# Routing the first 12 token tiles during attention and running four expert slots beside the routing of all tokens

## The chip, the cores and the metric

The kernel runs on one core of one Trainium2 chip. The metric is the device time of one execution in microseconds; the kernel before took 2799.47 us (median of three runs, 2798.77 to 2800.43). The core's engines are TensorE (PE in the profile), VectorE (DVE), ScalarE (ACT), GpSimd (POOL) and SyncE (SP), which here only issues DMAs. Each engine runs its own instructions in order and waits for others by semaphores.

## The reference

One image of 256 channels and 64 x 64 pixels goes through two layers: a windowed linear attention with a residual, and then, on its 4096 pixels as tokens, full attention with 8 heads and a mixture of experts. All is float32. The last part is the one that matters here:

```python
t = t + attn(layernorm(t))                 # 8 heads of 32, 4096 tokens
z = layernorm(layernorm(t))                # outer one is the expert's own, with gain and shift
logits = layernorm(t) @ Wr + br            # 8 experts
p, idx = top_k(softmax(logits), 2); w = p / p.sum()
y[e] = gelu((z * ln_g[e] + ln_b[e]) @ W1[e] + b1[e]) @ W2[e] + b2[e]   # 256 -> 1024 -> 256
out = t + w[0] * y[idx[0]] + w[1] * y[idx[1]]
```

Only the two chosen experts of each token count, so 8192 rows are computed instead of 32768.

## The kernel before

The tokens lie in 32 tiles of 128 (`t`, with eight more columns per token that hold the router's products). After the first layer, the part of the second layer that matters is in three stages.

**Attention.** 16 rounds (8 chunks of 512 queries, two groups of four heads), of 32 steps, one per tile of keys. In a step PE makes the scores of four heads (L1144) into one bank (`ps_one`) and a set of three banks (`three_banks`, two sets), ACT takes their exponentials (L1153, L1156) into one of eight weight buffers, and PE, two steps later, multiplies them with the values (L1103). DVE adds most weight buffers up for the denominators (`add`, L1175); every fourth step from 5 on a DMA from POOL's queue adds one instead (L1164). At given steps of a round other work is put in: `gather` at 5, `pack` at 9 (the last round's denominators, L1205, then DMAs on SP's queue), `turn` at 17, `spread` at 29, and in odd rounds from the third on two groups of output projections at 13 and 25 (`some_projections`, L1081), which also take a set of three banks, add to `t` (L1085) and make the statistics of the second norm (L151, L152). The whole stands in the true branch of a condition on the size of the scores; the false branch is a slower form of attention that these inputs do not take.

**Routing.** After the branch all 32 tiles are routed at once: two norms (ACT has the square roots), the normalised rows written to DRAM (`zrows`, L1398 on ACT and L1402 on SP), the logits and the two best experts on DVE (L1412 to L1433), counts before each token by two products on PE (L1436, L1438), and from these, on DVE, each token's position in its expert's list. Positions count in units of 128 rows; a slot is two units, 256 rows of one expert. The lists (which token stands at a position) come from an inversion: for each tile a one-hot matrix of positions within a unit (`line`, L1536) is multiplied with one of units (`piece`, L1538 to L1540), 64 products in 8 chunks (L1542). `owners` gives the expert of each slot (`expert_of`), and the last lines the row numbers to gather from (`source`) and to scatter to (`target`).

**Experts.** `run` goes through 32 slots of 256 rows and 4 of 128 (between them). For a slot, SP loads the expert's weights (L1366 to L1369, the expert's number read from `expert_of`), POOL issues gathers of the rows (L1582), PE transposes them (L1597), DVE applies gain and shift (L1601); then eight pairs of products with a Gelu each (L1622, L1625) and sixteen with the second layer's weights (L1631), DVE adds the bias (L1633) and POOL issues the scatters into `yrows` (L1634). The next slot's loads and transposes are issued one slot ahead. A conditional tail (`more_slots`) runs further single slots if the lists need them. A last stage weighs the two rows of each token, adds and transposes.

The order of instructions on each engine is made by a scheduler from the order in the code, dependences and its own estimates; `tc.issue_after(x)` holds an instruction behind another. Tiles of a later pool lie on memory of closed pools, and their first use waits for the last uses there.

Of the kernel before, what the change touches and what calls it, by code (L numbers as in the profile page):

```python
# [30 lines left out]
P = 128  # L31
# [18 lines left out]
NS = 2 * N // SLOT  # L50
NU = 2 * NS + NE
USUAL = 2 * NS + NE // 2
TAME = 60.0
# [9 lines left out]
    "m": {"rank": NE, "iota": P, "before": P, "ones": P, "number": 1, "high": 2 * NT, "spare": NU, "unit": NS + NE, "least": 2 * NE},  # L63
# [8 lines left out]
def constants():  # L72
# [32 lines left out]
    out[:, _AT["spare"]] = 1 + 2 * N + p[:, None] + P * np.arange(NU)[None, :]  # L105
    out[:, _AT["unit"]] = np.concatenate([2 * np.arange(NS), 2 * NS + np.arange(NE)])
# [5 lines left out]
def tile_conv_attn_hybrid(ctx: ExitStack, tc: tile.TileContext, a: dict, out: bass.AP):  # L112
# [771 lines left out]
    crows = e_dram.tile([NE, P, NH + 2 * KC], F32, name="crows")  # L884

# [13 lines left out]
    with ExitStack() as phase:  # L899
# [189 lines left out]
        with tc.If(tame > 0) as branch:  # L1089
            with (  # L1090
# [138 lines left out]

                def some_projections(n):  # L1230
                    tiles = list(range(len(done), len(done) + n))
                    done.extend(tiles)
                    pr = three_banks()
                    project([pr[:, j] for j in range(n)], tiles, lambda k, i: result(k, i // NB)[:, tok(i % NB)])

                for s, (r, i) in enumerate(places):
# [16 lines left out]
                    if s < len(places) - 2:  # L1253
                        add(r, i)

# [13 lines left out]
        with branch.Else():  # L1269


            with (
# [45 lines left out]
                for i in range(NT):  # L1318
                    project([ps.tile([P, CH], F32, tag="sc", name="ps_sc")], [i], lambda k, i: attnT[:, k, tok(i)])

# [5 lines left out]
    with ExitStack() as phase:  # L1326
# [7 lines left out]
        root = small.tile([1, 1], F32, name="root")  # L1334
        nc.scalar.sqrt(root, ident[:1, :1])
        cst.update(constants_of("m", wts))
        zrows = dram.tile([N, C], F32, name="zrows")
        yrows = dram.tile([2 * N + NU * P, C], F32, name="yrows")

# [12 lines left out]
        expert_of = small.tile([P, NS + NE], mybir.dt.int32, name="expert_of")  # L1352
# [4 lines left out]
        def weights(work, s):  # L1357

            e = nc.values_load(
                expert_of[:1, s : s + 1], engines=(mybir.EngineType.SP,), min_val=0, max_val=NE - 1  # L1360
            )
# [4 lines left out]
            nc.sync.dma_start(cols, crows[bass.ds(e, 1)].rearrange("o p n -> p (o n)"))  # L1366
            nc.sync.dma_start(w1, a["L1_ffn_W1"][bass.ds(e, 1)].rearrange("o (k p) h -> p (o k) h", p=P))
            nc.sync.dma_start(w2, a["L1_ffn_W2"][bass.ds(e, 1)].rearrange("o (k p) d -> p (o k) d", p=P))
            nc.sync.dma_start(b2, a["L1_ffn_b2"][bass.ds(e, 1)].rearrange("o d -> (o d)").partition_broadcast(P))  # L1369
# [5 lines left out]
        slot_work = experts.enter_context(tc.tile_pool(name="m_work", bufs=2))  # L1375

        with ExitStack() as routing:
            pool = lambda name, bufs: routing.enter_context(tc.tile_pool(name=name, bufs=bufs))
            r_ps = routing.enter_context(psum("r_ps", 2))
# [3 lines left out]


            norm = norm2
            norm.begin(0, NT)
            norm.end(0, NT)
            again = one("again")
            nc.vector.tensor_mul(again, norm.var, norm.rstd)
            nc.vector.tensor_mul(again, again, norm.rstd)  # L1390
            again = rstd_of(small, again, NT, 1e-5)
            nc.vector.tensor_mul(again, again, norm.rstd)
            less = one("less")
            nc.vector.scalar_tensor_tensor(less, norm.mean, -1.0, again, op0=ALU.mult, op1=ALU.mult)

            z = act.rearrange("p k n -> p (k n)").rearrange("p (i c) -> p i c", c=C)
            for i in range(NT):
                nc.scalar.activation(  # L1398
                    z[:, i, :], t[:, i, :C], AF.Identity, scale=again[:, i : i + 1], bias=less[:, i : i + 1]
                )  # L1400
                if i % 8 == 7:
                    nc.sync.dma_start(  # L1402
                        zrows[P * (i - 7) : P * (i + 1), :].rearrange("(i p) c -> p i c", p=P),
                        z[:, i - 7 : i + 1, :],
                    )

            on_experts = lambda v: v.unsqueeze(2).to_broadcast([P, NT, NE])
            on_tiles = lambda v: v.unsqueeze(1).to_broadcast([P, NT, NE])  # L1410
            logit = each("logit")
            nc.vector.tensor_mul(logit, on_experts(norm.mean), on_tiles(wr_sum))  # L1412
            nc.vector.tensor_sub(logit, t[:, :, C:], logit)
            nc.vector.tensor_mul(logit, logit, on_experts(norm.rstd))
            nc.vector.tensor_add(logit, logit, on_tiles(br))

            rank = on_tiles(cst["rank"])
            hots, most = [], [one(f"most{n}") for n in range(2)]
            for n in range(2):
                first, hot, place = each(f"first{n}"), each(f"hot{n}"), one(f"place{n}")  # L1420
                hots.append(hot)
                nc.vector.tensor_reduce(most[n], logit, AX.X, ALU.max)
                nc.vector.tensor_tensor(first, logit, on_experts(most[n]), ALU.is_equal)
                nc.vector.tensor_mul(first, first, rank)
                nc.vector.tensor_reduce(place, first, AX.X, ALU.max)
                nc.vector.tensor_tensor(hot, first, on_experts(place), ALU.is_equal)
                if n == 0:

                    nc.vector.scalar_tensor_tensor(logit, hot, -1e30, logit, op0=ALU.mult, op1=ALU.add)


            chosen = small.tile([P, NE, NT], F32, name="chosen")
            nc.vector.tensor_add(chosen.rearrange("p e i -> p i e"), hots[0], hots[1])  # L1433
            flat = lambda v: v.rearrange("p e i -> p (e i)")
            counts = bank()
            nc.tensor.matmul(counts[:, : NE * NT], cst["before"], flat(chosen), start=True, stop=True)  # L1436
            sums = bank()
            nc.tensor.matmul(sums[:, : NE * NT], cst["ones"], flat(chosen), start=True, stop=True)  # L1438
# [4 lines left out]
            nc.vector.tensor_copy(flat(per_tile), sums[:, : NE * NT])  # L1443
# [3 lines left out]


            iota = cst["iota"]
            total = upto[:, :, NT - 1]  # L1450
# [27 lines left out]

# [3 lines left out]
            nc.vector.tensor_scalar_mul(begins, begins, float(P))  # L1482

            def owners():


                past = small.tile([P, NS + NE, 2 * NE], F32, name="past")
                nc.vector.tensor_tensor(
                    past,
                    cst["unit"].unsqueeze(2).to_broadcast([P, NS + NE, 2 * NE]),  # L1490
                    ends.rearrange("p n e -> p (n e)").unsqueeze(1).to_broadcast([P, NS + NE, 2 * NE]),
                    ALU.is_ge,
                )
                owner = small.tile([P, NS + NE], F32, name="owner")
# [8 lines left out]
            by_tile = lambda v: v.unsqueeze(2).to_broadcast([P, NE, NT])  # L1503
            rest = small.tile([P, NE, NT], F32, name="rest")
# [3 lines left out]
            nc.vector.tensor_add(row, row, rest)  # L1508

# [5 lines left out]
            back = bank("acc")  # L1518
            for n in range(2):
                at = each(f"at{n}")  # L1520
                nc.vector.tensor_mul(at, hots[n], row.rearrange("p e i -> p i e"))
                pos = one(f"pos{n}")
                nc.vector.tensor_reduce(pos, at, AX.X, ALU.add)
                whole, part = (small.tile([P, NT], I32, name=f"{x}{n}") for x in ("whole", "part"))
                which, within = (small.tile([P, NT], BF16, name=f"{x}{n}") for x in ("which", "within"))
                nc.vector.tensor_copy(whole, pos)
                nc.vector.tensor_single_scalar(part, whole, P - 1, op=ALU.bitwise_and)
# [188 lines left out]
```

## Time and profile before

| | |
|---|---|
| median of three runs | 2799.47 us |
| the profiled execution, its own time | 2798.76 us |
| its span | 2797.0 us |
| PE busy | 2658.0 us (95%) |
| DVE busy | 1855.3 us (66%) |
| ACT busy | 1516.9 us (54%) |
| POOL busy | 812.0 us (29%) |
| last attention instruction on DVE ends | 2212.3 us |
| first product of an expert slot | 2262.6 us |

A busy share is of the whole span. A timeline line has start, length, engine, line of the code, operation, tiles (out<-in), shapes and how many instructions were merged; in brackets the idle time of the engine before it and what ended it. "issue" is idle time for which the profile shows no cause. A window line gives the busy time of each engine in a stretch, the clock that TensorE was granted (1.00 is full), the busy share of the DMA engines and the bytes moved.

### The profile page before, as it was taken

The numbers are of one execution on the slowest core, as the hardware profiler recorded it, in microseconds if no ns is written. First come the engines' busy times: TensorE is split into PE (matmuls) and PEld (weight loads), VectorE is DVE, ScalarE is ACT, GpSimd is POOL, SyncE is SP. The second block draws the span as 40 slices with busy tenths as digits, with TensorE's granted clock in tenths as the row PEclk, the third lists the DMA queues.
The fourth block names the chain that finished last, engine by engine and source line by source line (L and its number), as shares of the span: only waits on it lengthen the run. The fifth ranks groups of instructions, "written<-read, shape, count | busy, mean of one in ns | idle before, by whom it ended". The sixth has DMA issues, their size and how long they took to land.

```text
span 2797.0 us, 72047 instructions
## 1 busy us (share of the span) xinstructions
PE 2658.0 (95%) x31078; PEld 1216.5 (43%) x31078; DVE 1855.3 (66%) x2434; ACT 1516.9 (54%) x2117; POOL 812.0 (29%) x914
## 2 busy tenths in 40 slices
PE   6889999998999999999999999999999689999996
PEld 5454336645433655111212122222222168888884
DVE  6758788575878876888888888888888721111114
ACT  3222323222332334999898989999999622222222
POOL 2057777305777741100000000000000022222220
PEclk9999999999999999999999999999999889999997
DMA  5000000000000000555555555555555356656665
GB/s 143 6 23 25 11 28 21 8 12 23 25 11 28 21 21 2 112 120 113 109 120 109 118 111 111 111 118 109 120 109 113 94 185 208 198 197 199 208 214 191
DMA packets 120587, 265.77 MB, mean 95 GB/s; under 512 B 20386, under 2 KB 81416, under 8 KB 106180
## 3 DMA queue, kind: packets, MB, share of 16 engines
q0 software_dynamic: 22368, 133.18, 22.4%
q1 hardware_dynamic: 90724, 118.95, 13.1%
q10 hardware_dynamic: 7168, 8.92, 0.9%
q8 instruction: 248, 4.06, 0.6%
q14 instruction: 79, 0.65, 0.1%
HBM read 127.56 MB, written 18.12 MB: 52 GB/s over the span
## 4 chain that ended last, share of the span: by engine, by line
PE 92%; DVE 3%; issue 2%; DMA 2%; ACT 0%; POOL 0%; SPq 0%; ACTq 0%; DVEq 0%; POOLq 0%
PE ps_three L1144 18%; PE ps_acc L1103 18%; PE ps_hp L1622 8%; PE ps_yp L1631 8%; PE ps_sc L817 8%; PE ps_acc L833 7%; PE ps_sc L717 3%; PE ps_sc L744 3%; PE ps_acc L775 3%; PE ps_two L402 2%; PE ps_two L435 2%; PE ps_mm L988 2%; PE ps_two L516 1%; PE ps_acc L763 1%; PE ps_three L1081 1%
## 5 line engine op out<-in xcount | busy, mean ns | idle before, releaser
L1144 PE MATMUL ps_three<-qk 32*64 32x512 f32 x6144 | 563.3, 612 | 2.2 <-DVE t L1085 1.2
L1144 PE MATMUL ps_one<-qk 32*64 32x512 f32 x2048 | 556.7, 613 | 0.2 <-ACT pe L1153 0.2
L1175 DVE TENSOR_TENSOR act<-act,pe 128x2048 f32<-128x2048 f32 x195 | 446.8, 2291 | 97.2 <-ACT pe L1156 62.5
L637 ACT COPY sm<-ps_sc 128x384 f32<-128x384 f32 (+3 forms) x454 | 218.4, 510 | 527.2 <-PE ps_sc L817 338.8
L1156 ACT ACTIVATE pe<-ps_three 128x1536 f32<-128x1536 f32 x330 | 477.4, 1447 | 0.0
L644 DVE TENSOR_TENSOR sm<-ps_sc,mask 128x512 f32<-128x512 f32 (+3 forms) x740 | 340.1, 519 | 68.9 <-PE ps_sc L817 65.7
L644 POOL TENSOR_TENSOR sm<-sm,mask 128x192 f32<-128x192 f32 (+3 forms) x428 | 349.7, 846 | 113.9 <-ACT sm L637 113.6
L1175 DVE TENSOR_TENSOR act<-act 128x2048 f32<-128x2048 f32 x150 | 343.8, 2292 | 56.0 <-ACT act L1156 42.5
L1164 POOL DMA_DIRECT2D pe<-pe x108 | 92.9, 860 | 954.0 <-ACT pe L1156 666.7
L1103 PE MATMUL ps_acc<-pe,v 128*32 128x512 f32 x2640 | 351.6, 605 | 0.0
L1625 ACT ACTIVATE hid<-ps_hp,cols 128x256 f32<-128x256 f32 (+1 forms) x288 | 133.0, 462 | 360.4 <-PE ps_hp L1622 359.3
L1144 PEld LDWEIGHTS ps_three<-qk 32*64 32x64 f32 x6144 | 112.6, 129 | 414.9 <-ACT pe L1153 244.0
L1156 ACT ACTIVATE act<-ps_three 128x1536 f32<-128x1536 f32 x182 | 263.1, 1446 | 0.0
L1622 PE MATMUL ps_hp<-xe,w 128*128 128x256 f32 (+1 forms) x1152 | 246.1, 370 | 0.0
L1631 PE MATMUL ps_yp<-w,hid 128*128 128x256 f32 x1088 | 240.8, 379 | 0.0
L817 PE MATMUL ps_sc<-qk 32*64 32x384 f32 (+3 forms) x3584 | 234.6, 458 | 0.1
L1153 ACT ACTIVATE pe<-ps_one 128x512 f32<-128x512 f32 x330 | 197.3, 598 | 59.5 <-PE ps_one L1144 35.2
L644 POOL TENSOR_TENSOR sm<-sm,ycut 128x384 f32<-128x384 f32 (+4 forms) x146 | 147.2, 1029 | 256.8 <-ACT sm L637 256.5
L1622 PEld LDWEIGHTS ps_hp<-xe,w 128*128 128x128 f32 x1152 | 200.9, 190 | 39.4 <-ACT hid L1625 5.3
L1631 PEld LDWEIGHTS ps_yp<-w,hid 128*128 128x128 f32 x1088 | 204.2, 190 | 26.4
L833 PE MATMUL ps_acc<-sm,v 128*32 128x256 f32 (+3 forms) x2688 | 213.2, 419 | 0.1
L1601 DVE TENSOR_SCALAR xe<-ps_tp,cols 128x256 f32<-128x256 f32 (+1 forms) x72 | 34.8, 525 | 240.8 <-PE ps_tp L1597 217.1
(270 smaller groups left out, 3008.0 us busy)
## 6 DMA issues: line engine op xcount, KB each, us to landing
pe<-pe POOLq DMA_DIRECT2D x108, 1024.0 KB, 7.4
w<-in_L_ffn_W SPq DMA_DIRECT2D x72, 1024.0 KB
by<-recs SPq DMA_DIRECT2D x48, 256.0 KB
b<-in_L_ffn_b SPq DMA_DIRECT2D x36, 128.0 KB
rows<-in_x SPq DMA_DIRECT2D x16, 256.0 KB
zrows<-act SPq DMA_DIRECT2D x4, 1024.0 KB
y<-yrows ACTq DMA_DIRECT2D x8, 512.0 KB
y<-yrows SPq DMA_DIRECT2D x8, 512.0 KB
```

The costliest lines, as they stand in the source:

```text
L637: copied = nc.scalar.copy(sm[:, :used], sc[:, :used])
L644: done = engine.tensor_mul(to, of, mk.unsqueeze(1).to_broadcast(list(to.shape)))
L817: nc.tensor.matmul(scs[h][u : u + rows, at : at + n], kT[hs[h], P * i + u : P * i + u + rows], qT[hs[h], CH * ix + CELL * c0 : CH * ix + C ...
L833: nc.tensor.matmul(acc[hs[h], CELL * c0 : CELL * c1], v[:, i, hs[h]], sms[h][:, at : at + n], start=not begun[0], stop=last and at == plac ...
L1103: nc.tensor.matmul(to[D * hd : D * (hd + 1), :], lhsT(hd), rhs(hd), start=start, stop=stop, skip_group_check=True,)
L1144: nc.tensor.matmul(to[CELL * u : CELL * (u + 1), :], qk[hs, 1, g, P * i + CELL * u : P * i + CELL * (u + 1)], qk[hs, 0, g, chunk(qc)], sta ...
L1153: first = nc.scalar.activation(head(pe, 0), one, AF.Exp, scale=C**-0.5)
L1156: nc.scalar.activation(pe[:, CH:], three.rearrange("p h n -> p (h n)"), AF.Exp, scale=C**-0.5).ins
L1175: latest[:] = [nc.vector.tensor_add(total, total, weights_of[r, i]).ins]
L1622: nc.tensor.matmul(hp[:, :n], w1[:, k, tok(m)], x_now[:, k, :n], start=k == 0, stop=k == KC - 1)
L1625: nc.scalar.activation(hid[:, m, :n], hp[:, :n], AF.Gelu, bias=cols[:, m : m + 1])
L1631: nc.tensor.matmul(yp, hid[:, m, tok(j)], w2[:, m, :], start=m == 0, stop=m == NH - 1)
```

## The change

Three things change together.

A function `early_routing` routes the first 12 tiles and only for experts 0 to 3, in 18 parts that are put at steps of attention's rounds 8 to 14, each behind DVE's latest addition. It works in the memory of queries that those rounds no longer need. It makes `lists`, the rows of the first 256 tokens of each of the four experts, and writes the normalised rows of these tiles to `zrows`. Inverse square roots are made on DVE by an integer guess and three Newton steps (`rsqrts`) in place of ACT's square root, here and in the full routing.

The expert stage then has 4 early slots (experts 0 to 3, number known while the program is written), 28 full and 4 half slots. `run` has become a generator that stops after each pair of first-layer products and each half of second-layer products, and the routing code advances it in between: slot 0 up to the counts, slot 1 up to the inversion, slot 2 through the inversion, a piece after each chunk. The remaining 20 tiles' rows are scaled on ACT after the Gelus of slots 0 to 2 (`beside`). Early slots have gain and shift applied by ACT instead of DVE.

The full routing leaves out the rows that the early slots have taken (`gone`), and the sigmoid of the two weights is taken after the last Gelu.

```diff
+EARLY = 4
+ETILES = 12
-NS = 2 * N // SLOT
+NS = 2 * N // SLOT - EARLY
...
+    def rsqrts(x, y, part):
+        bits = y.bitcast(I32)
+        nc.vector.tensor_single_scalar(bits, x.bitcast(I32), 1, op=ALU.arith_shift_right)
+        nc.vector.tensor_scalar(bits, bits, -1.0, float(0x5F3759DF), op0=ALU.mult, op1=ALU.add)
+        for _ in range(3):
+            nc.vector.scalar_tensor_tensor(part, y, -0.5, y, op0=ALU.mult, op1=ALU.mult)
+            nc.vector.tensor_mul(part, part, x)
+            nc.vector.scalar_tensor_tensor(y, part, 1.5, y, op0=ALU.add, op1=ALU.mult)
...
+    def early_routing(spaces, banks):
...
+        def count():
+            of = banks(2)
+            for z, by in zip(of, ("before", "ones")):
+                nc.tensor.matmul(z[:, : E * M], c[by], flat(chosen), start=True, stop=True)
...
+        def invert():
+            (z,) = banks(1)
+            for n in range(2):
+                for i in range(M):
+                    nc.tensor.matmul(
+                        z[:, : 4 * E].rearrange("p (m n) -> p m n", m=2),
+                        line[n][:, :, i],
+                        piece[n][:, 1:, :, i],
...
+        def scaled(i):
+            to = staged[i // 2 % 2]
+            for j in range(2):
+                at = slice(i + j, i + j + 1)
+                nc.vector.tensor_scalar(
+                    to[:, j], t[:, i + j, :C], y[:, 1, at], less[:, at], op0=ALU.mult, op1=ALU.add
+                )
+            nc.sync.dma_start(zrows[P * i : P * (i + 2), :].rearrange("(i p) c -> p i c", p=P), to)
+
+        parts = [load, norms, top_one, top_two, count, ranks, lambda: place_of(0), lambda: place_of(1)]
+        parts += [lambda: one_hots(0), lambda: one_hots(1), invert, finish]
+        parts += [lambda i=i: scaled(i) for i in range(0, M, 2)]
+        return parts
...
+                spaces = [qk[:, 0, g, : 4 * CH] for g in range(KC)]
+                early = early_routing(spaces, some_banks)
+                when = [(8, 13), (8, 21), (8, 25), (9, 9), (9, 21), (10, 9), (10, 13), (10, 21), (10, 25), (11, 9), (11, 21), (12, 9)]
+                when += [(12, 13), (12, 21), (12, 25), (13, 9), (13, 21), (14, 9)]
...
+                    if (r, i) in early:
+                        with tc.issue_after(latest[0]):
+                            early[r, i]()
...
+                rows, n = (lists[:, 0], P * ETILES) if slot[0] is not None else (source, N)
...
+                    if by_scalar:
+                        nc.scalar.activation(
+                            xe[:, k, :n], tp[:, k, :n], AF.Identity, scale=cols[:, gain], bias=cols[:, shift]
+                        )
...
+                    if beside and (slot[0] or m >= NH // 2):
+                        with tc.issue_after(done["gelu"]):
+                            beside.pop(0)()
+                    yield
...
+        usual = [(e, 2 * e, 2 * e + 1) for e in range(EARLY)]
...
+            two_norms(0, NT, x, y, part, less)
+            rstd, again = y[:, 0], y[:, 1]
+            advance(1)
...
+            beside.extend(lambda i=i: scaled(i) for i in range(ETILES, NT))
...
+            advance(9)
...
+            with tc.issue_after(done["product"]):
+                nc.tensor.matmul(counts[:, : NE * NT], cst["before"], flat(chosen), start=True, stop=True)
+                nc.tensor.matmul(sums[:, : NE * NT], cst["ones"], flat(chosen), start=True, stop=True)
...
+            with tc.issue_after(done["y"]):
+                nc.vector.tensor_copy(flat(per_tile), sums[:, : NE * NT])
...
+            advance(10)
...
                     if n == 0 and i8 == G:
                         with tc.issue_after(made.ins):
                             owners()
-
+                    advance(1)
+
+            advance(2)
...
+        for _ in work_on:
+            pass
         experts.close()
+        with tc.issue_after(done["gelu"]):
+            for n in range(2):
+                nc.scalar.activation(top[n], top[n], AF.Sigmoid)
```

## The prediction, made before the result

> **What bounds the kernel now.** I read the slices first, then windows of 10 us where the slices dip, then the timeline there, and last the timeline of attention. The slices (70 us each; the page's second part) show TensorE at nine tenths nearly everywhere, with a dip in the 32nd, where its clock is also down:
>
> ```profile
> PE   6889999998999999999999999999999689999996
> DVE  6758788575878876888888888888888721111114
> PEclk9999999999999999999999999999999889999997
> ```
>
> The windows over that dip: start and end, length, busy us of PE, weight loads, DVE, ACT, POOL (instructions in brackets), granted clock, DMA share, GB/s.
>
> ```profile
> 2210.00:2220.00 10.00, 0.62 (x3) 0.19 (x1) 6.70 (x28) 1.45 (x4) 0.04 (x1) 0.67 0.01 3
> 2220.00:2230.00 10.00, 2.05 (x4) 1.18 (x4) 7.31 (x25) 10.00 (x22) 0.00 (x0) 0.50 0.52 177
> 2230.00:2240.00 10.00, 3.87 (x15) 2.31 (x16) 9.27 (x29) 8.35 (x16) 0.00 (x0) 0.50 0.72 244
> 2240.00:2250.00 10.00, 10.00 (x39) 5.42 (x38) 7.02 (x14) 3.44 (x5) 0.00 (x0) 0.50 0.77 237
> 2250.00:2260.00 10.00, 4.36 (x17) 2.17 (x15) 1.90 (x10) 2.06 (x2) 3.63 (x4) 0.50 0.69 241
> ```
>
> For about 52 us, from 2210.6 to 2262.6, TensorE does only the routing's own small products, at half clock: a serial stage. The timeline (start, us, engine, line, operation, tiles; idle before and what ended it) gives its links:
>
> ```profile
> 2157.39 2.05 PE L1081 MATMUL ps_three<-wo,act 128*128 128x264 f32 x8
> 2212.01 0.30 DVE L152 BATCH_NORM_AGGREGATE ln_mv<-st 128x2 f32<-128x6 f32 x2
> 2215.23 0.18 DVE L1452 TENSOR_SCALAR steps<-cstm 128x16 f32<-128x16 f32 x1 [2.92 <-issue]
> 2223.28 1.19 PE L1436 MATMUL ps_mm<-chosen,cstm 128*128 128x256 f32 x2 [12.66 <-DVE chosen L1433]
> 2225.37 0.42 DVE L1443 COPY per_tile<-ps_mm 128x256 f32<-128x256 f32 x1 [2.19 <-PE ps_mm L1438]
> 2236.13 17.16 PE L1542 MATMUL ps_acc<-piece,line 128*128 128x144 bf16 x64 [10.80 <-ACT piece L1539]
> 2240.93 0.39 SPq L1367 DMA_DIRECT2D w<-in_L_ffn_W  x1
> 2255.45 1.07 POOL L1582 DMA_INDIRECT xs<-zrows,source  x1 [45.41 <-DMA w<-in_L_ffn_W]
> 2258.47 0.66 PE L1597 MATMUL ps_tp<-cst,xs 128*128 128x128 f32 x2 [5.18 <-DMA xs<-zrows,source]
> 2262.62 2.91 PE L1622 MATMUL ps_hp<-xe,w 128*128 128x256 f32 x8
> 2307.26 7.09 PE L1622 MATMUL ps_hp<-xe,w 128*128 128x256 f32 x32
> 2314.63 7.07 PE L1631 MATMUL ps_yp<-w,hid 128*128 128x256 f32 x32
> 2321.53 7.09 PE L1622 MATMUL ps_hp<-xe,w 128*128 128x256 f32 x32
> ```
>
> Attention's last statistics (2212.3), 2.9 us for DVE to leave the branch, DVE's top-two choice, counts on PE, positions on DVE, inversion on PE (8 chunks of 8 products), row lists, gathers, first expert slot at 2262.6. From there slots run back to back: 6.91 us for the first layer, 6.91 for the second, 0.44 for four transposes (2307.26 to 2321.53 is 14.27). The fifth slot begins at 2321.5; the forecast is where that point goes. The wait charged to a weight load at 2255.45 is really for the source list, which DVE wrote at 2254.4.
>
> [...] last product over at 2210.6, clock 0.87 in 2212 to 2214, then 0.50, and full again in 2264 to 2266, after the first products at 2262.6. [...] gathers land 2.7 us after issue in the gap, 6.0 us (median) in 2290 to 2700, where weights stream. [...]
>
> **Is the same work done?** The slots stay 36: 32 full and 4 half, now 4 + 28 + 4. I computed the routing from the reference's inputs: the first 12 tiles hold 409, 386, 382 and 383 rows for experts 0 to 3, so all four early slots are full; all tiles hold 1063, 1010, 1041, 992, 1033, 995, 1042, 1016. With 256 taken from the first four, the full slots end at unit 56 of 56 and the half ones at 60 of 60, so the conditional tail is not run, as before. So no expert work is saved; four slots change place.
>
> **Attention (rounds 8 to 14).** A round without projections takes 66.5 us (1397.6 to 1464.1, between two denominators), one with two projection groups 70.5. A group (L1081, 2.05 us of PE) thus costs 2.0: PE runs its scores and value products back to back (2.04 us a step), so PE work is added one to one. The change adds PE work at two of its 18 points: counts, four passes of 48 columns (estimate 0.1 to 0.2 each from the 0.25 of a 264-column pass: 0.5); and the inversion, 24 bf16 weight loads with 16 columns. A pair of the late inversion takes 0.268 us at half clock (17.16/64), so 0.134 at full, less for fewer columns: bounds 1.7 and 3.2, taken 2.1. Both hold a three-bank buffer until DVE copies it; the second group of the last odd round waited 1.3 so; taken 0.4 for both. DVE gets some 100 small instructions: 14 + 9 + 7 of 0.2 to 0.3, two 1536-column compares of 1.0, 12 row scalings of 0.4, about 22 us, at most 3.1 at one point. They hide in DVE's idle steps: every fourth step has no addition. The gather addition (2.28 us, L1195) already stands in such a step and costs the even rounds nothing, and at points from step 13 on a weight buffer is reused after five steps or more (10.2 us) of which ACT and DVE use 2.0 + 2.3. Bounds 0 and 8 us, taken 0. Without that cover it would be the 22. POOL gets two fills and a cast of 1536 elements (about 1.5 from the 1.04 of 1024) between accumulating-DMA issues of 0.86 each fourth step: 0. SP gets 8 more DMAs, the row writes standing before the denominators' DMAs, which have over 10 us to spare (L1216 to L1225). Sum: **3.0 us**, bounds 1.5 and 8.
>
> **After attention** (times of before's trace; the 3.0 comes last). The order of instructions and their semaphores show that constants, weights and gathers of slot 0 wait for attention's last DVE instruction, 2212.35. Weights: constants, columns, then w1 issued about 2213.7; before, w1 took some 4.3 us from issue by the bandwidth of each us; so about 2218.5 to 2219.5. It isn't last. Gathers: four at 1.3 us from 2212.7, then POOL fills two tiles and casts the counter (1.04), so the fifth goes at 2219.2. The scheduler put the third slot's first transposes (that fifth gather) ahead of slot 0's first product. Landing is 2.7 us if free, 6.0 beside weights; 4.3 MB stream until about 2227, so I take 5.3: 2224.5, and the first product at **2225** (bounds 2221.5 and 2228).
>
> Slot 0: 13.82 + 0.22 (late transposes) + 1.5 for products begun at half clock (bounds 0 and 2.5) = 15.5, to 2240.5. Early slots do their entry on ACT (four of 0.5) and one Gelu table load (1.28), before PE needs them. DVE: no square-root table now, 11 dependent small operations of 0.2 to 0.25 in place of it; chosen at about 2226.5 instead of 2223.2, long before its product, which now stands behind slot 0. Counts on PE: four passes of 0.22 = 0.9, to 2241.4.
>
> Slot 1: 13.82, plus 0.5 since ACT has Gelu 0.47 and a row scaling 0.49 for each 0.86 of PE: to 2255.7. DVE meanwhile: from the counts' copy to the positions 5.1 as before, 1.2 for six new small operations, 5.8 to two chunks, expert list at 2256.5, rows added. Chunks 0 and 1 are ready at 2253: a margin of 2.7.
>
> Slot 2 is mixed with the inversion on PE: 13.82 + 0.44 + 8 chunks of 1.07 (17.16/8 at half clock, halved) = 22.8, to 2278.5. Between the end of a chunk and the start of the one after next PE has 2.8 us; DVE and ACT need 2.1 for it (0.61 + 0.49 + 0.78 and waits): no stall (bounds 0 and 4).
>
> Slot 3: 14.27, to **2292.8**. The fifth slot's weights wait on SP behind the last row write (scaling over near 2271): there by 2276; its rows by about 2280; its transposes stand near 2285. So routing is hidden, by 5 us.
>
> With 3.0 of attention the fifth slot starts at 2295.8 instead of 2321.5: **25.7 us** earlier. Everything after keeps its pitch. The new sigmoid and its table load come after the last Gelu, under 7 us of products: 0, and 1.6 without that cover. Span 2797.0 - 25.7 = 2771.3; the profiled execution (2798.76) would read 2773.1, the median 2799.47 - 25.7 = **2773.8**.
>
> **Rivals.** (a) A stage in series after all: DVE, shared between routing and slots' results, or gathers and zrows writes late, hold up slot 2 or slot 4, or attention pays up to 8. Loss 7 to 17 of the 25.7: 2781 to 2791. For it: the second half of routing starts only after slot 0, and slot 2's chunks need DVE and ACT in turn; against: the margins 2.7 and 5 above. (b) Less is lost: gathers uncontended (2222), clock up at once, inversion near its floor: 25.7 + 3 + 1.5 + 1.5 = 32, or 2767, at best 2762. (c) Slower: each of the 18 points costs attention what a projection group does, 2.0 us or more, since DVE's delay passes to the buffers that ACT needs: 36 against the 28.7 won outside, 2807. It decides from 1.6 us a point; the gather addition speaks against it. (d) Counts differ and the tail of 12 single slots runs: at 7 to 8 us each about +90; the nearest total is 8 rows from its limit.
>
> **Chances.** My case (2766 to 2781) 0.72; (a) 0.15; (b) below 2766 0.07; (c) and (d) 0.04; no difference 0.02. The range 2764 to 2786 takes the likeliest whole, half of (a) and part of (b). Faster by over 0.2% (5.6 us, about what a measurement can tell from nothing) 0.94, within it 0.02, slower 0.04.
>
> **What would show it.** Right: rounds without added PE work stay at 66.5; about 3 us more over rounds 9 and 11; first slot product about 12.5 us after attention's last statistics, ended by a gather, not a weight; PE busy from there with the chunks inside slot 2; no PE wait before the fifth slot's transposes. Wrong: additions (L1175 before) delaying ACT in rounds 8 to 14; PE idle in slot 2 or before slot 4; the first product after 2230.

## The result, and the profile after

The changed kernel takes 2789.41 us (median of seven runs, 2786.52 to 2792.98) against 2798.77 us (2796.00 to 2800.43) for the kernel before beside it: a ratio of 0.9969, 95% interval 0.9957 to 0.998. It is faster, by about 9 us where 25.7 were forecast, and lies outside the range given (2764 to 2786).

The slices of its page (70 us each) look like those of before with the dip almost gone:

```profile
PE   6889999988999999999999999999999899999996
DVE  6758688565878875888888888898888741111114
PEclk9999999999999999999999999999999999999996
```

What is left of the dip is in slice 32, with TensorE at eight tenths instead of six. The windows over the same stretch as before (length, busy us of PE, weight loads, DVE, ACT, POOL, with instructions in brackets, then granted clock, DMA share, GB/s):

```profile
2210.00:2220.00 10.00, 8.45 (x72) 3.05 (x64) 5.27 (x8) 2.66 (x4) 0.00 (x0) 1.00 0.00 2
2220.00:2230.00 10.00, 2.02 (x8) 1.44 (x8) 6.32 (x28) 0.00 (x0) 4.15 (x4) 0.81 0.41 121
2230.00:2240.00 10.00, 3.40 (x11) 1.86 (x12) 7.92 (x21) 2.30 (x3) 6.38 (x11) 0.50 0.98 348
2240.00:2250.00 10.00, 10.00 (x41) 8.27 (x41) 0.00 (x0) 6.09 (x14) 0.00 (x0) 0.84 0.34 119
2250.00:2260.00 10.00, 10.00 (x48) 8.66 (x47) 4.04 (x17) 3.78 (x9) 1.02 (x1) 1.00 0.91 289
```

So the change does what it says: TensorE's gap after attention shrank from 52 us to the 18 between 2222 and 2240, and behind it PE is busy through. The gap ends where the timeline shows it (start, us, engine, line, operation, tiles; in brackets the idle time before and what ended it), and the slots follow:

```profile
2220.20 2.02 PE L1263 MATMUL ps_three<-wo,act 128*128 128x264 f32 x8 [0.36 <-DVE act L1461]
2231.69 1.00 POOL L1587 DMA_INDIRECT xs<-zrows,lists  x1 [0.16 <-issue]
2239.33 0.66 PE L1602 MATMUL ps_tp<-cst,xs 128*128 128x128 f32 x2 [3.69 <-DMA xs<-zrows,lists]
...
2255.54 0.59 PE L1715 MATMUL ps_mm<-chosen,cstm 128*128 128x256 f32 x2
2270.22 2.25 PE L1821 MATMUL ps_acc<-piece,line 128*128 128x144 bf16 x8
2272.29 1.04 PE L1632 MATMUL ps_hp<-xe,w 128*128 128x256 f32 x4
2301.18 7.12 PE L1632 MATMUL ps_hp<-xe,w 128*128 128x256 f32 x32
2315.48 7.09 PE L1632 MATMUL ps_hp<-xe,w 128*128 128x256 f32 x32
```

The last projection starts at 2220.20; the fifth gather is issued at 2231.69 and releases its transposes at 2239.33; the counts end the first slot at 2255.54; the third slot begins at 2270.22 with the first chunk of the inversion, and that chunk holds PE for 2.07 us, to 2272.29, at full clock; the fourth slot begins at 2301.18, the fifth at 2315.48.

The fifth slot came 6.05 us before the 2321.53 of the kernel before. But in this execution attention itself began 3.07 us later (first write of the denominators at 1197.22 instead of 1194.15), ahead of round 8, where the change first adds work. Counted from that write the fifth slot came 9.1 us earlier. Behind it nothing moved: 475.7 us to the end of the span against 475.5. So the missing 16.6 us of the 25.7 lie between, and the stages add up (us; attention is from the first write of the denominators to the start of the last projection):

| stage | forecast | measured | missing |
|---|---|---|---|
| attention, over the 1014.45 of before | 3.0 | 8.5 | 5.5 |
| last projection to first slot product | 16.4 | 19.6 | 3.2 |
| first slot, to the counts | 15.5 | 15.8 | 0.3 |
| counts and second slot | 15.2 | 14.7 | -0.5 |
| third slot, with the inversion | 22.8 | 31.0 | 8.1 |
| fourth slot | 14.3 | 14.3 | 0.0 |

Three stages carry it, and the experiments take them one by one. For attention, the distance between the denominators' writes of two rounds is the measure. For rounds 8 to 14, step 9 to step 9 of the next, before had 66.5, 70.5, 66.6, 70.6, 66.6, 70.6, 66.6; the changed kernel has 70.4, 73.1, 66.6, 72.9, 69.2, 70.6, 63.9. So 3.9 were lost in the first of them (norms and first choice), 2.6 in the second (counts), 2.3 in the fourth (inversion). The 2.5 in the fifth is no loss on PE: that write of denominators stood on SP's queue behind a write of rows, and the time comes back two intervals later (63.9 instead of 66.6).

In the first of these the timeline of the changed kernel shows what PE waited for:

```profile
1725.82 0.68 DVE L1369 COPY act<-ps_acc 128x512 f32<-128x512 f32 x1
1726.56 1.06 PE L1285 MATMUL ps_acc<-act,v 128*32 128x512 f32 x8 [2.27 <-DVE act L1369]
1729.29 1.94 PE L1285 MATMUL ps_acc<-pe,v 128*32 128x512 f32 x8
```

There is one bank for the sums of values. DVE has to copy it at the end of a round before PE may start the next sums, and DVE came 2.27 us late. Eight value products that take 1.07 us took 1.94 soon after: the granted clock was 0.50 in 1728 to 1730, and 1.00 again from 1732.

### The profile page after: what moved, and what is told of

Read it like the earlier page. It is cut to its first block, busy times and chain, and to the rows that moved or that the text cites. A ratio compares the mean times of both kernels' runs of the same rounds, so it can differ in the third digit from the quotient of the medians.

```text
span 2791.2 us, 72155 instructions
## 1 busy us (share of the span) xinstructions
PE 2666.9 (96%) x31106; PEld 1221.1 (44%) x31106; DVE 1873.2 (67%) x2518; ACT 1512.3 (54%) x2110; POOL 817.1 (29%) x918
## 3 DMA queue, kind: packets, MB, share of 16 engines
q0 software_dynamic: 22368, 133.18, 22.7%
## 5 line engine op out<-in xcount | busy, mean ns | idle before, releaser
L1285 PE MATMUL ps_acc<-act,v 128*32 128x512 f32 x1456 | 193.9, 604 | 2.3 <-DVE act L1369 2.3
```

The lines of the kernel that those rows point to most:

```text
L1285: nc.tensor.matmul(to[D * hd : D * (hd + 1), :], lhsT(hd), rhs(hd), start=start, stop=stop, skip_group_check=True,)
```

## The experiments

Times of single executions move by some us with the part ahead of attention, so stages are compared, and a whole time only where several runs stand behind it. In runs that leave this part of attention as the changed kernel has it, the second of the intervals above is 73.1 or 74.6, and the first 70.3 to 70.5 or 68.9; what sets these apart is the clock, and the last section shows it.

**Columns of the late inversion side by side.**

```
-piece = r_work.tile([P, 3, NPC, G], BF16, name="piece")
+piece = r_work.tile([P, 3, G, NPC], BF16, name="piece")
-    piece[:, 1:, :, i],        # moving operand: 144 columns, 16 bytes apart
+    piece[:, 1:, i],           # two runs of 72, side by side
```

(Of the three instructions that fill it, DVE's compare and DVE's product read their operands in the other order.)

> Late inversion with its moving operand laid out tile by tile: the 144 columns that one product streams lie side by side (two runs of 72) instead of 16 bytes apart; weights as before. Theory A (the stride of the moving operand makes a pair take 0.26 us): a chunk of eight pairs falls from 2.07 to about 1.1 us and the third slot from 30.96 to about 23 us; the fifth slot's first transposes come some 8 us earlier after the counts. Rival B (the strided weights do it): the third slot stays at 31.0. Rival C (a fixed pitch of a pair of weights and product of this size): stays at 31.0 too. If VectorE's strided writes make its chunks the bound instead, PE waits for the one-hots show up and the slot lies between.

The third slot of this kernel on PE, its first and third chunk and the start of the fourth slot:

```profile
2264.97 0.68 PE L1827 MATMUL ps_acc<-piece,line 128*128 128x144 bf16 x8
2265.48 1.08 PE L1632 MATMUL ps_hp<-xe,w 128*128 128x256 f32 x4
...
2270.03 0.72 PE L1827 MATMUL ps_acc<-piece,line 128*128 128x144 bf16 x8 [1.62 <-ACT piece L1824]
...
2288.41 7.44 PE L1632 MATMUL ps_hp<-xe,w 128*128 128x256 f32 x32
```

A chunk now holds PE for 0.51 us (2264.97 to 2265.48) instead of 2.07: 0.064 a pair, even less than the theory had. The slot takes 23.4 us instead of 31.0. It isn't 18.4 (14.3 and eight times 0.51), above all because PE now waits for the one-hots, 2.8 us in sum: DVE's compare, which reads 16 bytes apart here, takes 1.21 us instead of 0.45.

**Weights of the late inversion side by side.**

```
-line = r_work.tile([P, P, G], BF16, name="line")
+line = r_work.tile([P, G, P], BF16, name="line")
-    line[:, :, i],
+    line[:, i],
```

> Late inversion with its weights laid out tile by tile (128 columns side by side instead of 16 bytes apart); the moving operand as before. Theory A (moving operand): the third slot stays at 31.0 us and a chunk at 2.07. Rival B (weights): the chunk falls to about 1.1 us, the slot to about 23. Rival C (fixed pitch): 31.0 here and with the columns side by side.

```profile
2264.72 2.20 PE L1824 MATMUL ps_acc<-piece,line 128*128 128x144 bf16 x8
2266.74 1.04 PE L1632 MATMUL ps_hp<-xe,w 128*128 128x256 f32 x4
...
2298.77 5.34 PE L1632 MATMUL ps_hp<-xe,w 128*128 128x256 f32 x24
```

A chunk takes 2.02 us. The slot grew to 34.1: PE now waits for DVE's one-hots, 1.4 us in sum, and behind the second of these waits PE's f32 products took twice their time: six of them 2.56 us (2288.52 to 2291.08), 0.43 each against the 0.216 of a slot at full clock. The chunk just ahead of these, begun at 2286.07, took 2.05 us and the one behind them, begun at 2291.08, 2.06, so the clock, from those products an estimated half, made the chunks no slower. The weights' distance costs PE next to nothing (2.07 us against 2.02); the moving columns' distance is what costs.

**Columns 8 bytes apart.**

```
-G = 8
+G = 4        # sixteen chunks of four tiles
```

> Late inversion in chunks of four tiles instead of eight: the moving columns stand 8 bytes apart instead of 16 (the weights' too), the number of products is the same. A pair took 0.26 us at 16 bytes and 0.064 with the columns side by side. Theory (time per column grows with its distance): between these, about 0.13 us, so the third slot 4 us shorter than 31 if VectorE's sixteen shorter chunks keep up. Rival (any distance costs the same): 0.26.

```profile
2271.72 0.69 PE L1821 MATMUL ps_acc<-piece,line 128*128 128x144 bf16 x4
2272.23 1.91 PE L1632 MATMUL ps_hp<-xe,w 128*128 128x256 f32 x8
```

Four pairs in 0.51 us: 0.127 each. So a pair takes 0.064, 0.127 and 0.259 us with its moving columns 2, 8 and 16 bytes apart: twice and four times what it takes with them side by side. (The weights' columns are 8 bytes apart here too; the run before showed that their distance hardly matters.) The third slot took 22.7 us here, just what had been forecast for it, by way of another layout.

**Norms and first choice moved.**

```
-when = [(8, 13), (8, 21), (8, 25), (9, 9), ...
+when = [(8, 13), (8, 1), (9, 1), (9, 9), ...
```

and the two moved parts stand behind the copy of the sums of values instead of behind the last addition.

> Only two of VectorE's early parts change place: the norms of the twelve tiles go from step 21 of round 8 to its step 1, behind the copy of the accumulator, and the first choice goes from step 25 of round 8 to step 1 of round 9, also behind that copy; the loads stay at step 13. Theory (VectorE was late with the copy of the one accumulator bank at the end of round 8, and PE stood for it): the interval of that round goes from 70.4 to 66.5 us, and attention is shorter by 3.9. Rival (the loads and the counter's cast on POOL at step 13 cost it): it stays at 70.4. Rival (any 5.5 us of VectorE's work costs some 3.9 wherever it stands): the 3.9 shows up spread over the intervals of rounds 7 to 9.

The writes of the denominators that bound the interval, first of the changed kernel, then of this one:

```profile
1674.67 0.50 SPq L1389 DMA_DIRECT2D dens<-rec  x1
1745.11 0.50 SPq L1389 DMA_DIRECT2D dens<-rec  x1
```

```profile
1671.29 0.51 SPq L1389 DMA_DIRECT2D dens<-rec  x1
1737.81 0.50 SPq L1389 DMA_DIRECT2D dens<-rec  x1
```

The interval is 66.52 instead of 70.44. The loads and the counter's cast are still in it, and so is the first choice, now behind the copy (1720.56 to 1723.14, ahead of the write at 1737.81). The interval before it, which now holds the norms, is 70.47 as ever (70.46), and the one after it is 74.6, as in runs without the move. So the same 23 small instructions cost 3.9 us at steps 21 and 25, and nothing behind the copy, where DVE would have stood still: after that copy it waits (2.36 us at 1803 in the changed kernel), since steps 0 and 1 of a round have no addition.

**Counts and inversion beside the denominators.** At step 9 of each round a tile of three banks holds the denominators in one of them. The counts and the early inversion go into the other two.

```
 def pack(r):
-    den = three_banks()[:, 0]
+    room = three_banks()
+    den = room[:, 0]
     by_ones(den, buffers[sums_of[r, own]], True, True)
+    beside_den = early.pop((r + 1, 9)) if r + 1 in (10, 12) else None
+    if beside_den:
+        beside_den([room[:, 1], room[:, 2]])   # count, then invert
 ...
-    nc.vector.tensor_copy(counted[:, n], z[:, : E * M])
+    nc.scalar.copy(counted[:, n], z[:, : E * M])   # behind rec's copy
```

> Only where the early counts and the early inversion land: their products write the two free banks of the tile of three that holds the sums of the weights at step 9 of rounds 10 and 12, and ScalarE copies them out behind its copy of those sums, instead of a tile of three of their own and copies by VectorE at step 21 of rounds 9 and 11; the parts that use them move a few steps later with them. Theory (the score banks are two deep, and a third user of them makes ScalarE wait for a full turn; VectorE's late copy lengthens it): round 9's interval falls from 73.1 to 74.6 us to about 70.5, and round 11's from 72.9 to about 70.6; rounds 10 and 12, which take them in, grow by ScalarE's small copies and PE's products, 0.3 to 1.5 us in sum; attention is 4 to 6 us shorter. Rival (the parts of VectorE at step 9 of round 9 cost it, the second choice and its like): round 9's interval stays above 73.

The second interval falls to 70.9 (0.45 over before) and the fourth to 72.0 (1.4 over). About 70.5 and 70.6 had been expected, with PE's own products in the rounds after; they stand just ahead of the write that ends an interval, so they are in these. The rival is out, as the second interval did not stay above 73. Attention is 1017.9 us, so 5.1 shorter than in the changed kernel's profile; 1.5 of that is a first interval of 68.9, which this edit doesn't touch, and 3.6 is the edit's, just under the 4 to 6 expected.

**Only ScalarE's copies.** The same copies by ScalarE, but counts and inversion keep their places and a tile of three of their own.

```
+if (r, i) in ((9, 21), (11, 21)):
+    early[r, i](some_banks(2))
+    with tc.issue_after(emptied[-1]):
+        emptied.append(copies.pop(0)().ins)
```

> The early counts and the early inversion keep their place (step 21 of rounds 9 and 11) and a tile of three banks of their own, as in the changed kernel; only the copies out of it are ScalarE's, behind the exponentials of that step, instead of VectorE's behind its additions. Theory (most of the loss is VectorE's late copy, which holds one of the two tiles of three): round 9's interval falls from 73.1 to 74.6 us to under 72, and round 11's from 72.9 to under 72.4, of which 1.4 is PE's own 24 pairs. Rival (a third user of the two tiles costs a turn whoever copies): 72.5 or more in both; then only the free banks beside the sums of the weights save it.

Neither theory has both intervals. The second stays at 73.0: the counts cost 2.5 us whoever copies them, so it is the turn of the tile of three that costs. The fourth falls to 72.1, the same as beside the denominators: for the inversion VectorE's late copy was the loss beyond PE's own 1.4.

PE's timeline at the counts shows where the 2.5 go, first in the changed kernel, then in this one:

```profile
1771.11 0.65 PE L1014 MATMUL ps_three<-qk 128*128 128x48 f32 x4
1771.69 1.07 PE L1326 MATMUL ps_one<-qk 32*64 32x512 f32 x2
1773.69 0.68 PE L1326 MATMUL ps_three<-qk 32*64 32x512 f32 x6 [0.94 <-DVE qk L1016]
```

```profile
1764.39 0.65 PE L1013 MATMUL ps_three<-qk 128*128 128x48 f32 x4
1764.96 1.07 PE L1324 MATMUL ps_one<-qk 32*64 32x512 f32 x4
1765.96 1.05 PE L1283 MATMUL ps_acc<-pe,v 128*32 128x512 f32 x2
1766.94 1.10 PE L1324 MATMUL ps_three<-qk 32*64 32x512 f32 x12
1767.97 1.06 PE L1283 MATMUL ps_acc<-pe,v 128*32 128x512 f32 x6
```

The counts' own products take 0.57 us in both. In the changed kernel two of the first head's score products then run alone for 1.06 us, and PE waits 0.94 for DVE's copy: 2.6 in sum. With ScalarE's copies PE has no wait at all, but it makes the step in two halves, first one head and then the other three, and takes 4.0 us for it (1764.96 to 1768.96) instead of 2.04. One head's scores alone last 1.0 us, as long as those of all four heads side by side (1.04 in the changed kernel, 1783.83 to 1784.87). At the inversion the step stays whole. That fits the times: at the counts ScalarE still reads the other tile of three, for the step before, until 1765.56, while at the inversion PE's 24 pairs end (1905.63) after that reading (1905.20). This is read from the trace; no run tests it alone.

**Third slot's transposes held.**

```
 for j in range(len(xs)):            # in enter(), now inside
     for k in range(KC):             # tc.issue_after(last product of the slot before)
         nc.tensor.transpose(...)
```

> Only the order on PE at the first slot: the transposes of the second and third slot stand behind the 16 first products of the slot before, so that the first product waits for the first slot's own rows and weights alone. Theory (the third slot's gather decided): the first product comes 14.3 us after the last projection's start, when the first slot's rows are ready on ScalarE (2234.44 - 2220.20), instead of 19.6, so 5 us earlier; the rest of the slots keep their lengths. Rival (the first weight matrix lands no earlier than the fifth gather, both sharing the DMA engines): 18 to 19.6 us, and the wait shown ahead of the first product is that for the weights.

Last projection, and the first products, in this kernel:

```profile
2218.78 2.02 PE L1263 MATMUL ps_three<-wo,act 128*128 128x264 f32 x8 [0.36 <-DVE act L1461]
2233.78 9.86 PE L1633 MATMUL ps_hp<-xe,w 128*128 128x256 f32 x32 [0.70 <-ACT xe L1608]
2250.82 0.59 PE L1716 MATMUL ps_mm<-chosen,cstm 128*128 128x256 f32 x2
```

The first product comes 15.0 us after the last projection instead of 19.6, released by ScalarE's entry of the slot's own rows (gain and shift); neither the fifth gather nor the weights are in the way. Not all of it is kept: this first slot takes 17.0 us instead of 15.8. Both begin below full clock: the slot's 32 first-layer products, 6.91 us at full clock, take 9.70 here and 8.61 in the changed kernel. There the clock was 0.50 in 2240 to 2242 and 1.00 from 2244, some 4 us after the first product; here, from the 2.79 us lost, half clock is estimated to have lasted 5.6 us. To the counts 3.3 us are won.

**Weights lent.** Why did the fifth gather take 7.6 us where 5.3 was forecast? Here the second slot takes the first slot's two matrices, so that theirs are not loaded.

```
-w1 = work.tile(...); w2 = work.tile(...)      # and their loads
+if early == 1:
+    w1, w2 = lent                               # the first slot's
```

> The changed kernel with the second slot's two weight matrices (2 MB) not loaded: it computes expert 1's early tokens with expert 0's matrices, so those rows are not what the reference has. Theory (the fifth gather takes 7.6 us from its start to the transposes that it releases, against 5.35 for the first, because it shares the DMA engines with the second slot's weights): it falls to 5.5 us or less and the first slot's product comes 2 us or more earlier, 17.5 us after the last projection's start. Rival (the gathers are served one after the other and the fifth is late by its place in the queue, or by VectorE's and POOL's own work): it stays at 7 us or more and the first product at 19 us or more.

The gather took 8.4 us and the first product came at 20.2. That is the rival's number, but the run doesn't bear it out: the third slot's matrices had moved up on SP's queue and were issued at 2225.70, 1.1 us ahead of the gather. The stream had only changed its owner. So the next kernel lends them to three slots (`early in (1, 2, 3)`), so that no later slot's matrix is loaded beside the gather:

> The run that left out the second slot's matrices did not empty the DMA engines: the third slot's moved up into their place, issued at 2225.70, before the fifth gather at 2226.79, and that took 8.4 us. Here the second, third and fourth slot all use the first slot's matrices, so that no weights stream beside the fifth gather (the early rows of experts 1 to 3 are then not what the reference has). Theory (the stream of weights holds the fifth gather): from its start to its transposes 5.5 us or less, and the first product 17.5 us after the last projection's start or earlier. Rival (something else holds it): 7 us or more, first product at 19 or later.

```profile
2225.98 1.00 POOL L1594 DMA_INDIRECT xs<-zrows,lists  x1 [0.16 <-issue]
2231.35 0.66 PE L1609 MATMUL ps_tp<-cst,xs 128*128 128x128 f32 x2 [1.35 <-DMA xs<-zrows,lists]
```

The gather took 5.37 us, and the first product came 17.1 us after the last projection. So the later slots' matrices cost it 2.3 us. Even the 5.4 is not the gather without weights that had been intended: the first slot's own second matrix, issued at 2221.29, still came in beside it, and the DMA engines' busy share was nine tenths or more in every 0.7 us from 2222.7 to 2230.4.

**All together.** Two more parts, at step 25 of rounds 10 and 12, went behind the copy of the value sums as well. The first such kernel wrote the two scaled copies of the one-hot column by column, from a one-hot compared in the old layout:

```
+hit = r_work.tile([P, NPC, G], BF16, name="hit")
+piece = r_work.tile([P, 2, G, NPC], BF16, name="piece", bufs=3)
+nc.scalar.activation(piece[:, 0].rearrange("p g n -> p n g"), hit, ...)
+nc.vector.tensor_mul(piece[:, 1].rearrange("p g n -> p n g"), hit, ...)
```

> Everything that the runs before point to in one kernel: the norms and the first choice behind the accumulator's copy, counts and inversion beside the sums of the weights, the transposes held behind the first products, and the late inversion's 144 columns side by side, here with the one-hot compared in the old layout and only its two scaled copies written column by column, and three chunks in flight. If the gains add: 3.9 + 4 to 6 + 3.3 + 7.5 or a little more is 19 to 22 us under the changed kernel's 2789.4, so 2768 to 2771. If they overlap (an earlier end of one stage is waited away in the next, the lists of the later slots becoming late): 2775 or more, with PE waiting for rows ahead of the fifth slot's transposes.

Single run 2776.92 us. The gains of attention and of the first product were there, but the third slot took 33.9 us. The groups that fill `piece` (busy us, mean ns of one, idle before):

```profile
L1828 ACT ACTIVATE piece<-hit,cstm 128x576 bf16<-128x576 bf16 x8 | 21.9, 2864 | 5.0 <-DVE hit L1827 4.9
L1829 DVE TENSOR_TENSOR piece<-hit,high 128x576 bf16<-128x576 bf16 x8 | 21.2, 2698 | 0.0
L1831 PE MATMUL ps_acc<-piece,line 128*128 128x144 bf16 x64 | 6.6, 255 | 10.0 <-DVE piece L1829 6.9 <-ACT piece L1828 3.1
```

576 elements written 144 bytes apart take 2.7 to 2.9 us, against 0.46 and 0.77 in the changed kernel, and PE waits for them. The second such kernel turns that around, for DVE's product too: it writes in order and reads 16 bytes apart.

```
-nc.scalar.activation(piece[:, 0].rearrange("p g n -> p n g"), hit, ...)
+nc.scalar.activation(piece[:, 0], hit.rearrange("p n g -> p g n"), ...)
```

> As the kernel with everything in it, but the late inversion's columns are written in order and the one-hot is read 16 bytes apart, where that kernel wrote them 144 bytes apart. There the two scaled copies took 2.70 us on VectorE and 2.86 us on ScalarE per chunk, PE waited 11.4 us for them in the third slot, and the slot took 33.9 us. Theory (the order of writing cost that): the copies fall to about 0.76 and 0.78 us as in the run that only laid the columns side by side, VectorE needs 0.69 + 0.45 + 0.76 = 1.9 us per chunk against PE's 2.3, and the third slot takes 22 to 24 us; the whole comes 20 to 22 us under the changed kernel, 2767 to 2770 us, about 0.989 of the kernel before. Rival (three chunks in flight or the held transposes cost it): the third slot stays over 28 us and the whole at 2775 or more.

```profile
L1828 ACT ACTIVATE piece<-hit,cstm 128x576 bf16<-128x576 bf16 x8 | 10.5, 1340 | 4.8 <-DVE hit L1827 4.8
L1829 DVE TENSOR_TENSOR piece<-hit,high 128x576 bf16<-128x576 bf16 x8 | 9.5, 1194 | 0.0
L1831 PE MATMUL ps_acc<-piece,line 128*128 128x144 bf16 x64 | 5.6, 230 | 2.2 <-DVE piece L1829 1.7 <-ACT piece L1828 0.3
```

The two copies take 1.34 and 1.19 us, more than the 0.78 and 0.76 expected, but PE's waits for them fall to 2.2 us and the third slot to 22.8. The whole takes 2766.67 us (median of four runs, 2766.47 to 2769.21) against 2796.9 for the kernel before: 0.9891 of it, interval 0.9875 to 0.9908, some 22 us better than the changed kernel by the two ratios. Its stages: attention 1.0 us over before, first product 14.2 us after the last projection, first slot 17.3, counts and second slot 15.1, third slot 22.8, fourth 14.3. The fifth slot comes 28.3 us earlier than before, counted from the first write of the denominators, and PE waits for nothing ahead of its transposes. That is 19.1 us better than the changed kernel's 9.1; the four changes alone had won 3.9, 3.6, 3.3 and 7.5, in sum 18.3. The gains add.

## Why the prediction missed

The course of events was right, and so was the sign. TensorE works from the first slot on, the inversion runs inside the third slot, the fifth slot's rows and weights are there in time, nothing moves behind it, and no tail runs. Four terms of the sum were too small, and together they make up the missing 16.6 us. In the first two it was not only the size: the reason given for it was wrong.

1. **The chunk of the inversion** (8.1 us of the 16.6). The step that failed is "17.16/8 at half clock, halved". A pair took 0.268 us at half clock before and takes 0.259 at full clock: the time was never the clock's. It belongs to the 144 moving columns, 16 bytes apart, as the three runs on the layout show. From the 0.064 of a pair with its columns side by side at full clock, half the clock alone would make an estimated 0.128; the row showed twice that, so something else than the clock set it. The prediction's own windows held a sign that these products are not like a slot's: PE was busy all through 2240 to 2250 and the clock stayed at 0.50, while behind the first slot's product at 2262.62 it was 0.66 in 2264 to 2265 and 1.00 in 2265 to 2266.

2. **DVE's parts in attention "taken at 0"** (3.9). The bounds 0 and 8 held it, the value did not. The argument, that every fourth step has no addition and weight buffers are reused late, was about the additions and the weights. It left out the copy of the one bank of value sums, with no spare at a round's end. 5.5 us of work at steps 21 and 25 had only the idle time of the few steps left. PE's wait was 2.3 of the 3.9, and the clock's fall behind it the rest. Where the work stands decides: moved behind the copy, it costs nothing. The prediction had named the sign, rounds without added PE work at 66.5; this one took 70.4.

3. **Banks for counts and inversion, "taken 0.4 for both".** PE's own part was sized well for the counts, 0.45 (0.5 forecast), and too large for the inversion, 1.4 (2.1, bounds 1.7 and 3.2). The third user of the two tiles of three cost 2.1 more for the counts, mostly the first head's scores made apart from the others and PE's wait of 0.94, and DVE's late copy 0.9 more for the inversion. In sum the stage lost 2.6 + 2.3 = 4.9 against 3.0 forecast.

4. **The fifth gather, "so I take 5.3"** (2.3 of the 3.2; it was also issued 0.9 later after the last projection). It took 7.6, beside weights: the two runs with lent weights put it at 8.4 with a later slot's matrices on their way and 5.4 without them. The right question had been asked (2.7 free, 6.0 under weights), but a value in between was taken although the weights were forecast to stream for longer than the gather needs. That the fifth gather decides at all was right, and the held transposes show it: without it the first product comes 4.6 us earlier.

The first slot (0.3), the second (0.5 not needed) and the fourth were right within half a us. Of the rivals, (a) came nearest: attention paid 8.5, just over its bound, and the time is inside (a)'s 2781 to 2791. But the largest loss has another cause than (a) gave: the third slot was lengthened by PE's own products, not held up by DVE, ACT or late rows, so that (a)'s range was hit in part by luck. Rival (c), each of the 18 points costing 2 us, is refuted: most cost nothing, and what was lost came in three places.

## To carry to other kernels

When a stage is moved under other work, ask of each duration what sets it before scaling it: compare the time of the row with that of the same product with its operands side by side, and if it is longer, as here (0.259 us against 0.064 at full clock), look at the strides. Count a busy engine's spare time up to its next deadline, not as a share of the stage, and look for the tiles that have only one bank. Where products run side by side, as four heads do here, see that added work doesn't pull them apart: PE then shows no wait and still takes twice as long (4.0 us against 2.04). A gather took 7.6 to 8.4 us here while the next slots' weights came in and 5.4 without those, so keep it off the first product's path by order.

## What the hardware showed that was not expected

- The distance of the moving columns of a bf16 product: 144 columns and a load of 128 weights take 0.064 us at 2 bytes, 0.127 at 8, 0.259 at 16, at full clock; and 0.268 at 16 bytes with half the clock. The distance of the weights' columns (16 or 2 bytes) made next to none (a chunk of 2.07 or 2.02).
- 576 bf16 elements on DVE: a product with everything 2 bytes apart takes 0.46 us, reading 16 bytes apart 1.19, writing 144 bytes apart 2.70. ScalarE's scaled copy: 0.77, 1.34 and 2.86.
- A step of attention whose four heads were made in two halves took PE 4.0 us instead of 2.04, without any wait in its timeline.
- A wait of PE of 2.3 us cost 3.9 in the changed kernel's profile: the clock was 1.00 in 1724 to 1726, 0.50 in 1728 to 1730 and 1.00 again from 1732, and the interval was 70.4; in the run with the columns 8 bytes apart, with the same wait (2.29 us), the clock stayed at 1.00 and the interval was 68.9. So the same wait came once with the fall and once without; what decides it was not shown. At the counts the fall came behind a shorter wait: behind PE's wait of 0.95 us the clock was 0.50 in 1768 to 1770 in the run with the two moved parts, and the interval 74.6; in the changed kernel it stayed at 1.00 (1772 to 1780) behind a wait of 0.94, and the interval was 73.1.
